# Token mean of the last image on TensorE, and a fixed VectorE order in the choice of experts

## Chip, cores and metric

The kernel runs on one core of a Trainium2 chip. The metric is the device time of one launch in microseconds; the times given are medians over runs. The profile is of one execution, and its times count from the start of its span.

## What is computed

Eight images of 32x32 pixels with 256 channels go through two layers. Layer 0 adds to each image a 3x3 convolution (192 channels) beside an attention with relative positions (64 channels), both of the group-normalised image. Layer 1 is a one-head attention over the 1024 tokens of an image, and then a mixture of experts. What matters here is the seam between those two: the token mean of each normalised image chooses two of eight experts for it.

```python
t = t + _L1_attn_ref(_ln_t(t), ...)
t = t + _L1_ffn_ref(_ln_t(t), ...)
# in _L1_ffn_ref, x being the normalised tokens:
logits = jnp.mean(x, axis=1) @ Wr + br
routing_weights = softmax(logits)
expected_loads = routing_weights.sum(axis=0) * (N / B)
scale = where(expected_loads > capacity, capacity / expected_loads, 1.0)
routing_weights = softmax(routing_weights * scale)
top_w, top_i = top_k(routing_weights, 2); top_w = softmax(top_w)
h = gelu(x @ W1[e] + b1[e]); y = h @ W2[e] + b2[e]
out = layernorm(sum of top_w * y over the two experts + x) * gamma + beta
```

`expected_loads` sums over all eight images, so no image's experts are known before the last image has left the attention of layer 1.

## The kernel before, in words

**Part one** (lines 92 to 1023) goes image by image. An image is a tile `T[b]` of 128 partitions with 8 token groups of 256 channels. `conv_layer_attention` and `attention_layer` do layer 0 and the attention of layer 1; while one image is in `attention_layer`, `fill` feeds TensorE with products of the next image. The last image has no next one, so its `fill` is empty. From line 971 on only TensorE's order is the order in the source (`tc.manual_schedule(engines={PE})`, line 971). On VectorE (DVE), ScalarE (ACT), GpSimd (POOL) and the DMA queues the order is planned at compile time from the dependencies: an instruction whose inputs are ready may be placed ahead of earlier lines. The order is then fixed in the program, and each engine takes its instructions one after the other.

At the end of `attention_layer` for image `b`, `gather` (line 863) and `project` (lines 872 to 881) finish the tokens of the last two groups, and `bn_stats`/`bn_aggr` leave each token's mean and variance in `mv2[:, b, t, :]`. Lines 903 to 909 turn the variances into 1/deviation (`tensor_scalar`, `Sqrt` on ACT, `reciprocal`) and form `mr`, mean times 1/deviation. The token sum `acc`, weighted with 1/deviation, is made by POOL for images 0 to 6 (line 915) and by DVE for image 7 (lines 919 and 921: one `tensor_scalar` and seven `scalar_tensor_tensor` over 256 channels). `T[b]` is stored to `Td[b]` (line 922). `token_mean` (lines 925 to 935) sums `acc` over the partitions with four TensorE passes (line 929, two fp32 products of two passes each), sums `mr` with another product (line 932), reduces it (line 934) and writes the mean, by channel, to `meanT[:, :, b]` (line 935). For images 0 to 6 this runs during the next image; for image 7 it stands alone.

`tab` is a 128x1 tile that serves only to load ACT's function tables early: line 653 computes a `Sqrt` of a late probability tile into it, line 767 an `Exp` of the freshly made deviations.

**The choice of experts** (lines 1054 to 1148) is a chain of tiny operations over 8 images x 8 experts. `plog` is the product with `Wr` (line 1056). `softmax` (lines 1060 to 1069) is a maximum, a subtraction, an `Exp` on ACT, a reciprocal and a multiplication; it is called three times (`sm1`, `sm2`, `sm3`). `pload` sums the loads over the images (line 1075). Then for each of two experts (lines 1092 to 1111): maximum, candidate indices (two operations), minimum, index (line 1099), one-hot row `oh`, the picked weight (lines 1104 and 1105), and the removal of the winner (lines 1108 and 1110). `prow` (line 1120) brings the indices onto one partition, line 1128 casts them to `idx_i`, from which the SP queue reads the addresses for the experts' weights (lines 1155 to 1169). `diag`, `pw` and `wbc` spread the experts' weights over the partitions (lines 1123, 1124, 1130); `dense`, `ptr`, `hotT`, `dbc` (lines 1132 to 1140) make what the biases need, and `pb`, `b1c` (lines 1144, 1148) gather the first bias. All of `plog`, `pload`, `prow`, `pw`, `ptr`, `pb` and later `tp2` take turns in one PSUM pool of two buffers (`ps_t`, tag "t").

**Part two** (lines 1177 to 1256) goes image by image: `load_image` reads `Td[b]` back (line 1152), `n2` normalises it on DVE (line 1189, eight operations of 128x256), TensorE transposes `n2` (line 1196), DVE and ACT copy that to `n2T` (lines 1200 and 1202), TensorE multiplies with `W1` (line 1220), ACT applies `Gelu` (line 1227), TensorE multiplies with the weighted `W2` (line 1237), and DVE and POOL finish the layer norm. Only POOL has its order fixed there.

Of the kernel before, what the change touches and what calls it, by code (L numbers as in the profile page):

```python
# [27 lines left out]
E, F = 8, 512  # L28
NF = F // P
TOPK = 2  # L30
IB = 256
NIB = IB // P
# [4 lines left out]
def kernel(  # L37
# [26 lines left out]
    nc = tc.nc  # L64
# [27 lines left out]
    with ExitStack() as ph:  # L92
        wp = ph.enter_context(tc.tile_pool(name="wp", bufs=1))
        work = ph.enter_context(tc.tile_pool(name="work", bufs=1))
# [25 lines left out]
        def st_tile(name):  # L120
            return ps_st.tile([P, 512], FP, tag="st", name=name)
# [3 lines left out]
        for n, table in (("h", key_rel_h), ("w", key_rel_w)):  # L125
# [21 lines left out]
            out=taps.rearrange("p (n o) -> p n o", o=CO), in_=conv_w.rearrange("a b (k p) o -> p (a b k) o", p=P)  # L147
# [36 lines left out]
        tab = wp.tile([P, 1], FP, tag="tab", name="tab")  # L184
# [573 lines left out]
        def attention_layer(b, fill, whole):  # L758
# [32 lines left out]
            for i in range(2):  # L791
                for q in range(2):
                    pq = st_tile("pq")
                    for kc in range(KC):
                        nc.tensor.matmul(
                            pq,
                            lhsT=wqkv1[:, i, kc, :],
                            rhs=nT[:, kc, q * 512 : (q + 1) * 512],
                            start=kc == 0,
                            stop=kc == KC - 1,  # L800
# [5 lines left out]
            for q in range(2):  # L806
                pv = st_tile("pv1").rearrange("p (j u) -> p j u", u=U)
                for j in range(4):
                    t = q * 4 + j
                    for kc in range(KC):  # L810
                        nc.tensor.matmul(
                            pv[:, j, :],
                            lhsT=nT[:, kc, t * P : (t + 1) * P],
                            rhs=wqkv1[:, 2, kc, :],
                            start=kc == 0,
                            stop=kc == KC - 1,
# [9 lines left out]
            pts = {}  # L826
            st2 = work.tile([P, NT, 6], FP, tag="lst", name="lst2")

            def scores(i):
                lg = lg_tile("lg1")  # L830
                for h in range(2):
                    nc.tensor.matmul(  # L832
                        lg[:, h, :],
                        lhsT=qk[0][:, i * P : (i + 1) * P],
                        rhs=qk[1][:, h * 512 : (h + 1) * 512],
                        start=True,
                        stop=True,
                    )
                lg = lg.rearrange("p h k -> p (h k)")
                nm = work.tile([P, 1], FP, tag="nm", name="nm", bufs=4)  # L840
                nc.vector.tensor_reduce(nm, lg, AX.X, ALU.max, negate=True)  # L841
                nc.vector.tensor_scalar(nm, nm, scale, None, ALU.mult)
                nc.scalar.activation(prs[:, i % 4, :], lg, AF.Exp, bias=nm, scale=scale, accum_out=rs[:, i, :])
# [56 lines left out]
                project(ib, os)  # L900


            m = mv2[:, b]
            rs2 = m[:, :, 1:2]
            nc.vector.tensor_scalar(rs2, rs2, 1e-5, None, ALU.add)
            nc.scalar.activation(rs2, rs2, AF.Sqrt)
            nc.vector.reciprocal(rs2, rs2)
            mr = work.tile([P, NT], FP, tag="mr", name="mr")
            nc.vector.tensor_tensor(mr, m[:, :, 0], m[:, :, 1], ALU.mult)
            acc = work.tile([P, C], FP, tag="n", name="acc", bufs=2)  # L910
            if b + 1 < B:
                part = work.tile([P, C], FP, tag="n", name="part", bufs=2)
                for t in range(NT):
                    to = part if t else acc
                    nc.gpsimd.tensor_scalar(to, T[b][:, t, :], m[:, t, 1:2], None, ALU.mult)
                    if t:
                        nc.gpsimd.tensor_tensor(acc, acc, part, ALU.add)
            else:
                nc.vector.tensor_scalar(acc, T[b][:, 0, :], m[:, 0, 1:2], None, ALU.mult)
                for t in range(1, NT):  # L920
                    nc.vector.scalar_tensor_tensor(acc, T[b][:, t, :], m[:, t, 1:2], acc, ALU.mult, ALU.add)
            nc.gpsimd.dma_start(out=Td[b], in_=T[b])
            return acc, mr

        def token_mean(b, acc, mr):

            pmt = st_tile("pmt")
            for kc in range(KC):
                nc.tensor.matmul(
                    pmt[:, kc : kc + 1], lhsT=acc[:, kc * P : (kc + 1) * P], rhs=ones[:, 0:1], start=True, stop=True  # L930
                )
            nc.tensor.matmul(pmt[:, KC : KC + NT], lhsT=ones, rhs=mr, start=True, stop=True)
            mrs = work.tile([P, 1], FP, tag="mrs", name="mrs")
            nc.vector.tensor_reduce(mrs, pmt[:, KC : KC + NT], AX.X, ALU.add)
            nc.vector.tensor_scalar(meanT[:, :, b], pmt[:, 0:KC], mrs, 1.0 / S, ALU.subtract, ALU.mult)

        class Conv:

# [106 lines left out]
    iota_i = small.tile([B, E], I32, tag="iota_i", name="iota_i")  # L1045
    nc.gpsimd.iota(iota_i, pattern=[[1, E]], base=0, channel_multiplier=0)
    iota = small.tile([B, E], FP, tag="iota", name="iota")
    nc.vector.tensor_copy(iota, iota_i)

    def sm(shape, name):  # L1050
        return small.tile(shape, FP, tag=name, name=name)
# [8 lines left out]
    def softmax(dst, src, name):  # L1060
# [7 lines left out]
        nc.vector.tensor_scalar(dst, dst, s, None, ALU.mult)  # L1068
        return d

    rw = sm([B, E], "rw")
    softmax(rw, logits, "sm1")

# [8 lines left out]
    z = sm([B, E], "z")  # L1082
# [8 lines left out]
    hot = []  # L1091
    for k in range(TOPK):
        m = sm([B, 1], f"m{k}")
        nc.vector.tensor_reduce(m, z, AX.X, ALU.max)
        cand = sm([B, E], f"cand{k}")
        nc.vector.tensor_scalar(cand, z, m, -float(E), ALU.is_equal, ALU.mult)
        nc.vector.tensor_tensor(cand, cand, iota, ALU.add)
        nc.vector.tensor_reduce(idx[:, k : k + 1], cand, AX.X, ALU.min)
        nc.vector.tensor_scalar(idx[:, k : k + 1], idx[:, k : k + 1], float(E), float(E - 1), ALU.add, ALU.min)
        oh = sm([B, E], f"oh{k}")  # L1100
        nc.vector.tensor_scalar(oh, iota, idx[:, k : k + 1], None, ALU.is_equal)
        hot.append(oh)
        pick = sm([B, E], f"pick{k}")
        nc.vector.tensor_tensor(pick, oh, rw2, ALU.mult)
        nc.vector.tensor_reduce(top[:, k : k + 1], pick, AX.X, ALU.add)
        if k + 1 < TOPK:
            off = sm([B, E], f"off{k}")
            nc.vector.tensor_scalar(off, oh, 4.0, None, ALU.mult)
            z2 = sm([B, E], f"z{k}")
            nc.vector.tensor_tensor(z2, z, off, ALU.subtract)  # L1110
            z = z2
    wt = sm([B, TOPK], "wt")
    softmax(wt, top, "sm3")


    prow = ps_t.tile([P, 512], FP, tag="t", name="prow")
    pw = ps_t.tile([P, 512], FP, tag="t", name="pw")
    diag = sm([B, TOPK, B], "diag")
    for k in range(TOPK):
        nc.tensor.matmul(  # L1120
            prow[0:1, k * B : (k + 1) * B], lhsT=idx[:, k : k + 1], rhs=ident[0:B, 0:B], start=True, stop=True
        )
        nc.vector.tensor_scalar(diag[:, k, :], ident[0:B, 0:B], wt[:, k : k + 1], None, ALU.mult)
    nc.tensor.matmul(
        pw[:, 0 : TOPK * B], lhsT=ones[0:B], rhs=diag.rearrange("p k b -> p (k b)"), start=True, stop=True
    )
    idx_i = small.tile([1, TOPK * B], I32, tag="idx_i", name="idx_i")
    nc.vector.tensor_copy(idx_i, prow[0:1, 0 : TOPK * B])
    wbc = sm([P, TOPK * B], "wbc")
    nc.vector.tensor_copy(wbc, pw[:, 0 : TOPK * B])  # L1130
    dense = sm([B, E], "dense")
# [14 lines left out]
        )  # L1146
    b1c = sm([P, NF, TOPK * B], "b1c")
    nc.vector.tensor_copy(b1c, pb)

    def load_image(b):  # L1150
        t = work.tile([P, NT, C], FP, tag="T2", name="T2")
        nc.sync.dma_start(out=t, in_=Td[b])
        return t

    def load_experts(b):
        ws = []
# [20 lines left out]
    ctx.enter_context(tc.manual_schedule(engines={mybir.EngineType.Pool}))  # L1177
    nxt = load_experts(0)
    scale_experts(0, nxt)
    tn = load_image(0)  # L1180
    for b in range(B):
        ws, Tb = nxt, tn
        if b + 1 < B:
            tn = load_image(b + 1)
            nxt = load_experts(b + 1)
        n2 = work.tile([P, NT, C], FP, tag="n2", name="n2")
        n2T = work.tile([P, KC, S], FP, tag="n2T", name="n2T")
        for t in range(NT):
            nc.vector.tensor_scalar(
                n2[:, t, :], Tb[:, t, :], mv2[:, b, t, 0:1], mv2[:, b, t, 1:2], ALU.subtract, ALU.mult  # L1190
            )
        for kc in range(KC):
            for q in range(2):
                tp = ps_t.tile([P, 4, P], FP, tag="t", name="tp2")
# [112 lines left out]
```

## Time and profile before

| | us |
|---|---|
| median of 3 runs (2446.56 to 2452.04) | 2448.43 |
| the profiled execution's own time | 2444.67 |
| its span | 2442.9 |
| TensorE busy in the span | 2314.1 (95%) |
| VectorE busy | 1485.5 (61%) |
| ScalarE busy | 1026.1 (42%) |
| GpSimd busy | 475.6 (19%) |

In the timeline a row gives the start, the busy time, engine and line, the operation with the tiles it writes and reads, how many were merged, and in brackets how long the engine was idle before it and whose result it waited for. "PE" is a matmul, "PEld" a weight load that overlaps it. An fp32 product appears as two passes ("x2"). In a table by stretches, each engine's busy time and its number of instructions stand side by side, then the clock that TensorE was granted (1.00 is full speed), the busy share of the DMA engines and GB/s.

### The profile page before, as it was taken

How to read it: one execution, taken by the hardware profiler on the slowest of the kernel's cores; microseconds unless marked ns; L12 is line 12 of the kernel's file. 1: busy time of each engine (PE TensorE's matmuls, PEld its weight loads, DVE VectorE, ACT ScalarE, POOL GpSimd, SP SyncE). 2: the span in 40 equal slices, each digit the busy share in tenths (PEclk: the TensorE clock that was granted, in tenths of full speed). 3: DMA queues.
4: the chain of work that ended last, by engine and by line, in shares of the span. 5: the costliest groups of instructions: out<-in, count | busy, mean ns of one | idle time of the engine just before them, and what ended most of it. 6: DMA issues, size and time to landing. Idle time of an engine off the chain costs nothing. (4 is left out here: it accounts for less than half of the span.)

```text
span 2442.9 us, 41840 instructions
## 1 busy us (share of the span) xinstructions
PE 2314.1 (95%) x17273; PEld 1299.7 (53%) x17273; DVE 1485.5 (61%) x2661; ACT 1026.1 (42%) x1717; POOL 475.6 (19%) x446
## 2 busy tenths in 40 slices
PE   5999999999999999999999999999998879999998
PEld 4535643564366436643663376337632546666665
DVE  7776487548755875587467746774774434444443
ACT  2255336433643464346335732563266323222232
POOL 3202130213031202210230023002301032222221
PEclk7999999999999999999999999999999989999999
DMA  4521242134222412240324032403240032121210
GB/s 124 82 40 27 41 97 39 35 46 90 32 43 57 80 22 51 57 85 9 58 70 72 4 57 70 72 4 57 60 66 2 23 121 69 69 69 69 70 60 26
DMA packets 71468, 135.82 MB, mean 56 GB/s; under 512 B 12000, under 2 KB 24168, under 8 KB 69232
## 3 DMA queue, kind: packets, MB, share of 16 engines
q1 hardware_dynamic: 65488, 115.47, 23.7%
q0 software_dynamic: 3056, 15.73, 1.9%
q8 instruction: 136, 2.23, 0.4%
q10 hardware_dynamic: 2736, 1.97, 0.3%
q14 instruction: 52, 0.43, 0.1%
HBM read 53.43 MB, written 25.17 MB: 32 GB/s over the span
## 5 line engine op out<-in xcount | busy, mean ns | idle before, releaser
L591 DVE TENSOR_REDUCE my<-lg 128x32 f32<-128x1024 f32 x512 | 618.5, 1223 | 161.8 <-PE st L623 125.9
L631 ACT ACTIVATE PT<-st 128x512 f32<-128x512 f32 (+1 forms) x944 | 541.6, 633 | 306.2 <-PE st L623 301.7
L623 PE MATMUL st<-F,km 32*128 32x512 f32 x2048 | 545.2, 641 | 17.2 <-DMA F<-mb 11.9
L583 PE MATMUL lg<-km,F 24*128 24x512 f32 x2048 | 534.9, 637 | 6.1 <-DMA F<-kq 3.7
L640 PE MATMUL po<-PT,vall 128*32 128x256 f32 (+1 forms) x3200 | 315.1, 453 | 2.9 <-ACT PT L631 2.4
L583 PEld LDWEIGHTS lg<-km,F 24*128 24x128 f32 x2048 | 156.0, 183 | 186.5 <-issue 112.1
L515 PE MATMUL pc<-convw,gdif 128*128 128x192 f32 x1152 | 236.1, 345 | 11.5 <-ACT m L524 8.7
L640 PEld LDWEIGHTS po<-PT,vall 128*32 128x32 f32 x3200 | 66.9, 108 | 314.6 <-issue 280.1
L515 PEld LDWEIGHTS pc<-convw,gdif 128*128 128x128 f32 x1152 | 186.8, 192 | 81.5 <-issue 59.9
L623 PEld LDWEIGHTS st<-F,km 32*128 32x128 f32 x2048 | 177.5, 184 | 96.3 <-issue 43.5
L1220 PE MATMUL phd<-n2T,w 128*128 128x512 f32 x512 | 223.7, 594 | 0.0
L1237 PE MATMUL py<-w,hT 128*128 128x256 f32 x1024 | 223.6, 379 | 0.0
L1237 PEld LDWEIGHTS py<-w,hT 128*128 128x128 f32 x1024 | 194.6, 190 | 33.3 <-issue 7.4
L311 POOL TENSOR_TENSOR T<-T,l0b 128x2048 f32<-128x2048 f32 x8 | 36.4, 4546 | 633.5 <-PE tpx L304 633.5
L1220 PEld LDWEIGHTS phd<-n2T,w 128*128 128x128 f32 x512 | 97.0, 191 | 114.9 <-issue 107.7
L1244 DVE TENSOR_TENSOR r<-py,n 128x256 f32<-128x256 f32 x64 | 27.1, 423 | 215.0 <-PE py L1237 215.0
L863 PE MATMUL po<-pt,qkv 128*128 128x256 f32 x512 | 116.6, 381 | 11.3 <-DVE pt L855 11.3
L524 ACT COPY m<-pc 128x384 f32<-128x384 f32 x48 | 23.0, 479 | 247.3 <-PE pc L515 247.3
L1227 ACT ACTIVATE hT<-phd,b1c 128x512 f32<-128x512 f32 x128 | 86.3, 686 | 96.5 <-PE phd L1220 96.3
L841 DVE TENSOR_REDUCE nm<-lg 128x1 f32<-128x1024 f32 x64 | 78.1, 1220 | 77.5 <-PE lg L832 77.5
L780 POOL TENSOR_TENSOR T<-T,n 128x256 f32<-128x256 f32 x64 | 47.1, 743 | 372.8 <-DVE n L775 372.8
L832 PE MATMUL lg<-qkv 128*128 128x512 f32 x256 | 119.1, 593 | 0.0
(250 smaller groups left out, 2627.6 us busy)
## 6 DMA issues: line engine op xcount, KB each, us to landing
F<-rh SPq DMA_DIRECT2D x256, 128.0 KB
F<-kq SPq DMA_DIRECT2D x256, 64.0 KB
F<-rwd SPq DMA_DIRECT2D x256, 64.0 KB
w<-in_L_ffn_W_dram SPq DMA_DIRECT2D x32, 512.0 KB
rwd<-rw SPq DMA_DIRECT2D x16, 512.0 KB
Td<-T POOLq DMA_DIRECT2D x8, 1024.0 KB, 8.3
T<-Td SPq DMA_DIRECT2D x8, 1024.0 KB
out_dram<-yo SPq DMA_DIRECT2D x16, 512.0 KB
```

Source lines behind the costliest of these rows:

```text
L515: nc.tensor.matmul(pc[:, v, :], lhsT=gflat[:, 2 * pair + v, kc, at : at + P], rhs=convw[:, 2 * pair + v, dy, kc * CO : (kc + 1) * CO], sta ...
L583: nc.tensor.matmul(lg[:, a, :], lhsT=self.F[r : r + 24, a, 0, i * P : (i + 1) * P], rhs=KM[self.g][r : r + 24, a].rearrange("p e k -> p (e ...
L591: nc.vector.tensor_reduce(my[:, :, hl], lg.rearrange("p a (y x) -> p y a x", y=WW), AX.XY, ALU.max)
L623: nc.tensor.matmul(st[:, i, :] if len(heads) > 1 else st, lhsT=KM[self.g][r : r + 32, a, e, :], rhs=self.F[r : r + 32, a, e, :], start=Tru ...
L631: nc.scalar.activation(self.pts[j][:, hs, :], st, AF.Exp)
L640: nc.tensor.matmul(self.po[32 * hl : 32 * hl + 32, cols], lhsT=vall[:, j, h * (DH + 1) : h * (DH + 1) + 32], rhs=self.pts[j][:, hl, cols], ...
L832: nc.tensor.matmul(lg[:, h, :], lhsT=qk[0][:, i * P : (i + 1) * P], rhs=qk[1][:, h * 512 : (h + 1) * 512], start=True, stop=True,)
L841: nc.vector.tensor_reduce(nm, lg, AX.X, ALU.max, negate=True)
L863: nc.tensor.matmul(po[:, 0:IB], lhsT=v1[:, jc, :], rhs=pt[:, jc, :], start=jc == 0, stop=jc == NT - 1)
L1220: nc.tensor.matmul(phd, lhsT=ws[k][0][:, kc, f * P : (f + 1) * P], rhs=n2T[:, kc, q * 512 : (q + 1) * 512], start=kc == 0, stop=kc == KC - 1,)
L1227: nc.scalar.activation(hT[:, k * NF + f, :], phd, AF.Gelu, bias=b1c[:, f, k * B + b : k * B + b + 1])
L1237: nc.tensor.matmul(py, lhsT=hT[:, k * NF + f, j * P : (j + 1) * P], rhs=ws[k][1][:, f, :], start=k == 0 and f == 0, stop=k == TOPK - 1 and ...
```

## The change

For image 7 the weighted token sum is a product on TensorE: token group as stationary operand, the column of 1/deviation as moving operand, summed over the eight groups in PSUM, in two halves of channels. The deviations are made in two parts, groups 0 to 5 and groups 6 and 7. After it an `Exp` from `tab` to `tab` stands in the source. `token_mean` writes `meanT` with one operation for each half of the channels, for all images. In the choice of experts, DVE's order is that of the source from the first softmax to `b1c`; the candidates take one operation instead of two, the removal of the winner one instead of two, the index is made after the one-hot row, the picked weights, `sm3`, `pw` and what follows stand after `idx_i` and after the normalisation of image 0, which is now called there. `load_image(0)` is called ahead of the first softmax.

```diff
+            def deviation(part):
+                m = mv2[:, b, part]
+                rs2 = m[:, :, 1:2]
+                nc.vector.tensor_scalar(rs2, rs2, 1e-5, None, ALU.add)
+                nc.scalar.activation(rs2, rs2, AF.Sqrt)
+                nc.vector.reciprocal(rs2, rs2)
+                nc.vector.tensor_tensor(mr[:, part], m[:, :, 0], m[:, :, 1], ALU.mult)
...
             if b + 1 < B:
+                deviation(slice(0, NT))
...
             else:
-                nc.vector.tensor_scalar(acc, T[b][:, 0, :], m[:, 0, 1:2], None, ALU.mult)
-                for t in range(1, NT):
-                    nc.vector.scalar_tensor_tensor(acc, T[b][:, t, :], m[:, t, 1:2], acc, ALU.mult, ALU.add)
+                acc = [st_tile(f"pm{kc}") for kc in range(KC)]
+                for part in (slice(0, NT - NIB), slice(NT - NIB, NT)):
+                    deviation(part)
+                    for t in range(part.start, part.stop):
+                        for kc in range(KC):
+                            nc.tensor.matmul(
+                                acc[kc][:, 0:1],
+                                lhsT=T[b][:, t, kc * P : (kc + 1) * P],
+                                rhs=mv2[:, b, t, 1:2],
+                                start=t == 0,
+                                stop=t == NT - 1,
+                            )
+                nc.scalar.activation(tab, tab, AF.Exp)
             nc.gpsimd.dma_start(out=Td[b], in_=T[b])
...
-            nc.vector.tensor_scalar(meanT[:, :, b], pmt[:, 0:KC], mrs, 1.0 / S, ALU.subtract, ALU.mult)
+            for kc in range(KC):
+                nc.vector.tensor_scalar(
+                    meanT[:, kc, b : b + 1], acc[kc][:, 0:1], mrs, 1.0 / S, ALU.subtract, ALU.mult
+                )
...
-    nc.vector.tensor_copy(iota, iota_i)
+    nc.vector.tensor_scalar(iota, iota_i, -float(E), None, ALU.add)
...
+    tn = load_image(0)
...
+    order = tc.manual_schedule(engines={mybir.EngineType.DVE})
+    order.__enter__()
     rw = sm([B, E], "rw")
     softmax(rw, logits, "sm1")
...
-        nc.vector.tensor_scalar(cand, z, m, -float(E), ALU.is_equal, ALU.mult)
-        nc.vector.tensor_tensor(cand, cand, iota, ALU.add)
-        nc.vector.tensor_reduce(idx[:, k : k + 1], cand, AX.X, ALU.min)
-        nc.vector.tensor_scalar(idx[:, k : k + 1], idx[:, k : k + 1], float(E), float(E - 1), ALU.add, ALU.min)
+        nc.vector.scalar_tensor_tensor(cand, z, m, iota, ALU.is_equal, ALU.mult)
+        low = sm([B, 1], f"low{k}")
+        nc.vector.tensor_reduce(low, cand, AX.X, ALU.min)
         oh = sm([B, E], f"oh{k}")
-        nc.vector.tensor_scalar(oh, iota, idx[:, k : k + 1], None, ALU.is_equal)
+        nc.vector.tensor_scalar(oh, iota, low, None, ALU.is_equal)
...
-            nc.vector.tensor_scalar(off, oh, 4.0, None, ALU.mult)
-            nc.vector.tensor_tensor(z2, z, off, ALU.subtract)
+            nc.vector.scalar_tensor_tensor(z2, oh, -4.0, z, ALU.mult, ALU.add)
             z = z2
+        nc.vector.tensor_scalar(idx[:, k : k + 1], low, float(E), float(E - 1), ALU.add, ALU.min)
...
+    nc.vector.tensor_copy(idx_i, prow[0:1, 0 : TOPK * B])
+    first = normalised(0, tn)
+    for k, oh in enumerate(hot):
+        nc.vector.tensor_tensor(pick, oh, rw2, ALU.mult)
+        nc.vector.tensor_reduce(top[:, k : k + 1], pick, AX.X, ALU.add)
+    softmax(wt, top, "sm3")
...
     b1c = sm([P, NF, TOPK * B], "b1c")
     nc.vector.tensor_copy(b1c, pb)
+    order.__exit__(None, None, None)
...
-    tn = load_image(0)
     for b in range(B):
...
+        n2 = normalised(b, Tb) if b else first
```

`normalised(b, Tb)` holds the eight operations that stood at line 1189. In `token_mean` the product of line 929 is kept for images 0 to 6; image 7 reads the two PSUM columns of the new product, and its `pmt` lies in the other PSUM pool (`lg_tile`).

More of the change, by code (lines that the diff above doesn't have):

```diff
@@ L827, in attention_layer @@
             st2 = work.tile([P, NT, 6], FP, tag="lst", name="lst2")
+            mr = work.tile([P, NT], FP, tag="mr", name="mr")
+            def deviation(part):
[5 more added lines that the diff above has]
+                nc.vector.tensor_tensor(mr[:, part], m[:, :, 0], m[:, :, 1], ALU.mult)
             def scores(i):
@@ L900, in attention_layer @@
                 project(ib, os)
[L903 to L910, printed above, removed]
             if b + 1 < B:
+                deviation(slice(0, NT))
+                acc = work.tile([P, C], FP, tag="n", name="acc", bufs=2)
                 part = work.tile([P, C], FP, tag="n", name="part", bufs=2)
@@ L914, in attention_layer @@
                     to = part if t else acc
-                    nc.gpsimd.tensor_scalar(to, T[b][:, t, :], m[:, t, 1:2], None, ALU.mult)
+                    nc.gpsimd.tensor_scalar(to, T[b][:, t, :], mv2[:, b, t, 1:2], None, ALU.mult)
                     if t:
@@ L925, in token_mean @@
         def token_mean(b, acc, mr):
[L927 to L931, printed above, removed]
+            pmt = lg_tile("pmt")[:, 0, :] if b + 1 == B else st_tile("pmt")
+            if b + 1 < B:
+                for kc in range(KC):
+                    nc.tensor.matmul(
+                        pmt[:, kc : kc + 1], lhsT=acc[:, kc * P : (kc + 1) * P], rhs=ones[:, 0:1], start=True, stop=True
+                    )
+                acc = [pmt[:, kc : kc + 1] for kc in range(KC)]
             nc.tensor.matmul(pmt[:, KC : KC + NT], lhsT=ones, rhs=mr, start=True, stop=True)
@@ L934, in token_mean @@
             nc.vector.tensor_reduce(mrs, pmt[:, KC : KC + NT], AX.X, ALU.add)
-            nc.vector.tensor_scalar(meanT[:, :, b], pmt[:, 0:KC], mrs, 1.0 / S, ALU.subtract, ALU.mult)
+            for kc in range(KC):
+                nc.vector.tensor_scalar(
+                    meanT[:, kc, b : b + 1], acc[kc][:, 0:1], mrs, 1.0 / S, ALU.subtract, ALU.mult
+                )
         class Conv:
@@ L1047, with load_image, normalised @@
     iota = small.tile([B, E], FP, tag="iota", name="iota")
-    nc.vector.tensor_copy(iota, iota_i)
+    nc.vector.tensor_scalar(iota, iota_i, -float(E), None, ALU.add)
+    def load_image(b):
+        t = work.tile([P, NT, C], FP, tag="T2", name="T2")
+        nc.sync.dma_start(out=t, in_=Td[b])
+        return t
+    def normalised(b, Tb):
+        n2 = work.tile([P, NT, C], FP, tag="n2", name="n2")
+        for t in range(NT):
+            nc.vector.tensor_scalar(
+                n2[:, t, :], Tb[:, t, :], mv2[:, b, t, 0:1], mv2[:, b, t, 1:2], ALU.subtract, ALU.mult
+            )
+        return n2
+    tn = load_image(0)
     def sm(shape, name):
@@ L1095 @@
         cand = sm([B, E], f"cand{k}")
-        nc.vector.tensor_scalar(cand, z, m, -float(E), ALU.is_equal, ALU.mult)
-        nc.vector.tensor_tensor(cand, cand, iota, ALU.add)
-        nc.vector.tensor_reduce(idx[:, k : k + 1], cand, AX.X, ALU.min)
-        nc.vector.tensor_scalar(idx[:, k : k + 1], idx[:, k : k + 1], float(E), float(E - 1), ALU.add, ALU.min)
+        nc.vector.scalar_tensor_tensor(cand, z, m, iota, ALU.is_equal, ALU.mult)
+        low = sm([B, 1], f"low{k}")
+        nc.vector.tensor_reduce(low, cand, AX.X, ALU.min)
         oh = sm([B, E], f"oh{k}")
-        nc.vector.tensor_scalar(oh, iota, idx[:, k : k + 1], None, ALU.is_equal)
+        nc.vector.tensor_scalar(oh, iota, low, None, ALU.is_equal)
         hot.append(oh)
-        pick = sm([B, E], f"pick{k}")
-        nc.vector.tensor_tensor(pick, oh, rw2, ALU.mult)
-        nc.vector.tensor_reduce(top[:, k : k + 1], pick, AX.X, ALU.add)
         if k + 1 < TOPK:
-            off = sm([B, E], f"off{k}")
-            nc.vector.tensor_scalar(off, oh, 4.0, None, ALU.mult)
             z2 = sm([B, E], f"z{k}")
-            nc.vector.tensor_tensor(z2, z, off, ALU.subtract)
+            nc.vector.scalar_tensor_tensor(z2, oh, -4.0, z, ALU.mult, ALU.add)
             z = z2
-    wt = sm([B, TOPK], "wt")
-    softmax(wt, top, "sm3")
+        nc.vector.tensor_scalar(idx[:, k : k + 1], low, float(E), float(E - 1), ALU.add, ALU.min)
     prow = ps_t.tile([P, 512], FP, tag="t", name="prow")
-    pw = ps_t.tile([P, 512], FP, tag="t", name="pw")
-    diag = sm([B, TOPK, B], "diag")
     for k in range(TOPK):
@@ L1122 @@
         )
+    idx_i = small.tile([1, TOPK * B], I32, tag="idx_i", name="idx_i")
+    nc.vector.tensor_copy(idx_i, prow[0:1, 0 : TOPK * B])
+    first = normalised(0, tn)
+    for k, oh in enumerate(hot):
+        pick = sm([B, E], f"pick{k}")
+        nc.vector.tensor_tensor(pick, oh, rw2, ALU.mult)
+        nc.vector.tensor_reduce(top[:, k : k + 1], pick, AX.X, ALU.add)
+    wt = sm([B, TOPK], "wt")
+    softmax(wt, top, "sm3")
+    pw = ps_t.tile([P, 512], FP, tag="t", name="pw")
+    diag = sm([B, TOPK, B], "diag")
+    for k in range(TOPK):
         nc.vector.tensor_scalar(diag[:, k, :], ident[0:B, 0:B], wt[:, k : k + 1], None, ALU.mult)
@@ L1126 @@
     )
-    idx_i = small.tile([1, TOPK * B], I32, tag="idx_i", name="idx_i")
-    nc.vector.tensor_copy(idx_i, prow[0:1, 0 : TOPK * B])
     wbc = sm([P, TOPK * B], "wbc")
@@ L1148 @@
     nc.vector.tensor_copy(b1c, pb)
[L1150 to L1153, printed above, removed]
+    order.__exit__(None, None, None)
     def load_experts(b):
@@ L1185 @@
             nxt = load_experts(b + 1)
-        n2 = work.tile([P, NT, C], FP, tag="n2", name="n2")
+        n2 = normalised(b, Tb) if b else first
         n2T = work.tile([P, KC, S], FP, tag="n2T", name="n2T")
[L1188 to L1191, printed above, removed]
         for kc in range(KC):
```

## Prediction

> **What bounds the kernel now.** First the page.
>
> ```profile
> span 2442.9 us, 41840 instructions
> PE 2314.1 (95%) x17273; PEld 1299.7 (53%) x17273; DVE 1485.5 (61%) x2661; ACT 1026.1 (42%) x1717; POOL 475.6 (19%) x446
> PEclk7999999999999999999999999999999989999999
> ```
>
> TensorE is the bound nearly everywhere. The change touches places where it isn't, so I cut the span into stretches of 40 us (columns: PE, PEld, DVE, ACT, POOL, then clock).
>
> ```profile
> 1920.00:1960.00 40.00, 26.54 (x128) 19.76 (x126) 22.14 (x64) 11.94 (x21) 0.74 (x2) 0.89 0.20 67
> 1960.00:2000.00 40.00, 31.80 (x110) 20.91 (x111) 13.97 (x59) 10.20 (x17) 20.56 (x8) 0.77 0.36 126
> 2000.00:2040.00 40.00, 40.00 (x149) 26.67 (x148) 16.41 (x37) 12.38 (x19) 5.51 (x3) 1.00 0.20 66
> ```
>
> From 2000 on PE is full up to the end, so whatever lets its stream of part two begin earlier is kept to the end. Between 1946 and 1969 it waits for a chain of small steps. The timeline there:
>
> ```profile
> 1941.23 3.72 PE L863 MATMUL po<-pt,qkv 128*128 128x256 f32 x16 [1.41 <-DVE pt L855]
> 1945.43 1.28 ACT L906 ACT_TABLE_LOAD   x1
> 1946.64 0.88 DVE L879 SCALAR_TENSOR_TENSOR T<-pa,rc,T 128x256 f32<-128x256 f32 x2 [5.37 <-PE pa L875]
> 1948.90 0.20 DVE L907 RECIPROCAL mv<-mv 128x8 f32<-128x8 f32 x1 [0.28 <-ACT mv L906]
> 1949.60 3.61 DVE L921 SCALAR_TENSOR_TENSOR acc<-T,mv,acc 128x256 f32<-128x256 f32 x7
> 1953.36 0.98 PE L929 MATMUL pmt<-ones,acc 128*128 128x1 f32 x4 [6.76 <-DVE acc L921]
> 1954.81 0.17 DVE L934 TENSOR_REDUCE mrs<-pmt 128x1 f32<-128x8 f32 x1 [1.60 <-PE pmt L932]
> 1956.47 1.28 ACT L1066 ACT_TABLE_LOAD   x1 [7.60 <-DVE sm_d L1065]
> 1960.93 0.41 DVE L1189 TENSOR_SCALAR n<-T,mv 128x256 f32<-128x256 f32 x1
> 1965.20 0.15 DVE L1128 CAST idx_i<-prow 1x16 int32<-1x16 f32 x1
> 1967.90 0.35 DVE L1123 TENSOR_SCALAR diag<-ident,wt 8x8 f32<-8x8 f32 x2
> 1969.26 1.88 PE L1144 MATMUL pb<-hotT,b1sb 8*128 8x16 f32 x8 [0.28 <-DVE hotT L1138]
> 1971.07 1.11 PE L1196 MATMUL tp<-ident,n 128*128 128x128 f32 x4
> ```
>
> Three pieces stand in the chain: the weighted sum on DVE (1949.2 to 1953.2), the table load ahead of the first exponential, and the choice. In the choice, normalisations of line 1189 are wedged between its steps: from 1960.93 to 1967.7 I count sixteen, image 0's eight and then image 1's. From `pb` at 1969.26 PE is busy without a pause. That start is what the change can move.
>
> The experts' weights aren't late: SP issues the first load 1.22 after `idx_i` (1966.57); by the DMA rates it lands around 1970.5, an estimate, and the product using it starts at 1975.0.
>
> **What the Trainium skill says.** "ScalarE: Activation LUTs", section "What ACT_TABLE_LOAD costs", gives 1283 ns for the load; the trace agrees (1.28). The page adds a drain of 1380 ns, which I don't see: the exponential starts at 1957.76, right behind the load. "TensorE: Matmul & The Clock Gate", section "LDWEIGHTS (loading the stationary operand)", lets a weight load depend on its columns alone, columns/1.2 ns, 107 for 128. The trace agrees at full clock:
>
> ```profile
> 1644.52 1.90 PE L417 MATMUL pvv<-qkvw,x 128*128 128x64 f32 x16
> ```
>
> With 0.275 for the last one that is 0.11 a pass; at half clock `pb` takes 0.235. The same page, "What's actually happening", halves the clock after an idle window of about 3.4 us. Here it falls at 1950.7, 4.1 after the last product of line 875, and is full again only at 1978.1.
>
> **Part 1, the mean by PE.** Removed: line 919 (0.35), line 921 (3.61) and line 929's four passes, 1953.36 to 1954.2. Added: 16 products, 32 passes, in PE's fixed order behind line 875. Groups 0 to 5 have their variances at 1941.26, and DVE and ACT idle then, so their deviations should be ready before PE is free at about 1946.4. Their 24 passes take 24 x 0.11 = 2.6, to 1949.05. Groups 6 and 7 follow the same DVE steps as now; reciprocal done at 1949.1. Eight passes, 0.9, to 1950.05, line 932's two with their tail 0.35: line 934 starts at 1950.45 instead of 1954.81. Minus 4.35. `meanT` takes a second small operation: plus 0.13 (two of line 1123 take 0.35). Net 4.2.
> Bounds: were the square root of the first part planned behind the copy of line 867, its table load ends at 1946.7 and I lose 0.8. Were the first part to wait for all eight variances, 32 x 0.11 = 3.5 begin at 1949.15 and the gain is 1.7. Were the clock to fall earlier, 0.11 becomes 0.235, the sum ends at 1953.9, line 932 takes 0.6, and the gain is 0.2.
>
> **Part 2, the table.** If the new `Exp` of `tab` runs after the second square root, the load of 1.28 at 1956.47 leaves the chain. But it reads only `tab`, last written at line 767 (1886.7); ACT's order isn't fixed, and ACT idles 1.90 just after. That the planner pulls ready work far ahead is seen in line 1189: image 1's normalisation, a whole image further down the source, runs inside the choice. I take it that the `Exp` goes up there, under a table that is Exp's anyway, and brings 0. Bounds: 0 and minus 1.3.
>
> **Part 3, the choice.** I count from the end of `sm2`'s subtraction, 1960.0, in steps seen undisturbed: 0.18 to 0.19 for a dependent small operation (1958.98 to 1959.78), 0.25 with a per-row scalar. The fixed order puts `sm2`'s reciprocal and scaling, which wait for ACT, ahead of the maximum: it starts at +0.79, now +0.03. Then five dependent steps for the first expert, to +1.90; four for the second, index ready at +2.73; `prow` and cast, `idx_i` at +3.25, now +5.35. So 2.1 earlier, but only for weights that aren't late.
> For `pb` the order costs: eight normalisations in a row, 2.7 (line 1189's group of eight at 2050.71 takes 2.67), to +5.95; picked weights 0.6; `sm3` with its ACT trip 1.25; `diag` at +7.8 (now +7.9). Then `wbc` is in front of `dense` and waits for `pw`, about 0.6, where `dense` now fills that wait; `dense`, `ptr`, `hotT` end at +9.8, `pb` starts at +9.86 instead of +9.26. Loss 0.6. PE's transposes don't get ahead: `tp2` shares the two PSUM buffers in turn, and even now `n2` of four groups is ready at 1962.7 while its transposes run at 1971.07.
> Queued behind: behind the cast sits DVE's normalisation, which needs image 0 back from `Td`. SP's load waited for the store (until 1952.6), then for `meanT` (1955.2); now the store is last, so it issues about 1952.7 and lands, by today's issue at 1955.37 and first use at 1960.93, by 1958.2 at the latest. It is wanted at 1959.05: no wait, 0.9 to spare; past that each us counts. SP's other DMAs keep their order: two image loads, then the experts; POOL's only change is `Td`'s store, still behind line 879.
> Image 1's eight normalisations lose their free place. They lie under TensorE's stream (DVE idles 18.5 before 1994.45), unless the planner puts some ahead of the copies of line 1200 or into the last steps: 0 to 2.7, I take 0.5.
>
> **Part 4, images 0 to 6.** One more small DVE operation each, 7 x 0.13 = 0.9 if DVE were the bound; PE is full there, so 0.2, bounds 0 and 0.9.
>
> **Sum.** 4.2 - 0.6 - 0.5 - 0.2 = 2.9 off the path. Against the profiled execution: 2444.67 to 2441.8, span 2442.9 to 2440.0. That execution is 3.8 below the runs' median; from 2448.43 the same step gives 2445.5.
>
> **Rivals.**
> A, likeliest, as summed: 2445.5.
> B, the table does come ahead: 1.3 more, 2444.2. For it: ACT also idles after the second root. Against it: nothing ties it there.
> C, the mean isn't ready early (dependency on all variances, or half clock): gain 1.7 or 0.2, about 1.0 for 4.2, leaves the total at about 2448.7, no change. For it: the clock falls at 1950.7, just behind my end of 1950.4.
> D, slower. Images differ now: line 907 comes every 239.1 for images 1 and 2 and every 237.5 for images 3 to 5. At the end of layer 0's attention the longer ones show a stretch at half clock:
>
> ```profile
> 442.00:444.00 2.00, 2.00 (x12) 0.25 (x10) 2.00 (x6) 1.94 (x4) 0.00 (x0) 0.53 0.00 0
> ```
>
> The extra operation and the new dependencies let the planner re-order DVE and ACT in images 0 to 6; if four more of them meet that, 4 x 1.6 = 6.4 against 2.9: 2451.9. It decides from two images on. Against it: PE's order is fixed there, and the change is tiny in that part.
>
> **Numbers.** A 0.46, B 0.29, C 0.15, D 0.10. What a measurement can tell from no change is about 0.2%, 4.9 us: below 2443.5 or above 2453.3. Medians of a few runs scatter by some 2 us (2446.56 to 2452.04 before). A falls below 2443.5 in 0.09 of its 0.46, B in 0.14 of 0.29, C in 0.02: faster 0.25. D is above 2453.3 in half of its 0.10, C and A in 0.01: slower 0.06. Within: 0.69. The range goes from B with the best mean and nothing lost in parts 3 (image 1) and 4 (gain 5.0 and one scatter: 2441.4) to C with a scatter (2450.7).
>
> **What would show it.** Right: line 934 about 4.3 earlier relative to line 879; a table load still in front of the first exponential of the choice; `idx_i` about 3.3 after `sm2`'s subtraction; `pb` about 9.9 after it. Wrong: no table load there (B); PE waiting for deviations or 0.2 a pass (C); DVE waiting for `T` from `Td`, or image 1's normalisations between `hotT` and the copies; longer periods of line 907 (D).

## The result, and the profile after

| | before | after |
|---|---|---|
| median, 22 runs each | 2451.10 | 2445.64 |
| lowest, highest | 2443.42, 2453.03 | 2440.24, 2449.88 |
| profiled execution's own time | 2444.67 | 2449.88 |
| its span | 2442.9 | 2448.1 |

The ratio is 0.9983 [0.9975, 0.9992]: the change takes off 4.2 us, between 2.0 and 6.1, by 2451.1. The runs of either kernel fall into groups: 2443.4 to 2443.8, 2446.5 and 2450.6 to 2453.0 before, 2440.2 to 2441.2, 2442.6 to 2444.2 and 2447.1 to 2449.9 after. Group against group the change brings about 3, and the medians differ by 5.5 because 13 of 22 runs before and 11 of 22 after lie in the highest group. The profiled execution after is its kernel's slowest run, so spans can't be compared. I compare the seam instead.

Lines have moved: 879 became 890, 934 became 950, 1066 became 1101, 1128 became 1151, 1189 became 1078, 1144 became 1183, 1196 became 1226, 1220 became 1250. First the page of the kernel after.

```profile
span 2448.1 us, 41896 instructions
PE 2325.5 (95%) x17301; PEld 1304.1 (53%) x17301; DVE 1482.9 (61%) x2661; ACT 1027.0 (42%) x1719; POOL 476.2 (19%) x446
PEclk7999999999999999999999999999999989999999
```

PE is busy 11.4 longer than before, far more than the 28 new records of passes can take. That is a clock, not work; I come back to it. Now the timeline of the seam after the change.

```profile
1950.07 0.21 ACT L836 ACTIVATE mv<-mv 128x6 f32<-128x6 f32 x1
1954.75 3.73 PE L929 MATMUL pm<-mv,T 128*128 128x1 f32 x32
1954.95 0.88 DVE L890 SCALAR_TENSOR_TENSOR T<-pa,rc,T 128x256 f32<-128x256 f32 x2 [4.25 <-PE pa L886]
1958.74 0.17 DVE L950 TENSOR_REDUCE mrs<-pmt 128x1 f32<-128x8 f32 x1 [1.18 <-PE pmt L948]
1958.94 0.34 DVE L952 TENSOR_SCALAR meanT<-pm,mrs 128x1 f32<-128x1 f32 x2
1960.27 1.28 ACT L1101 ACT_TABLE_LOAD   x1 [3.10 <-DVE sm_d L1100]
1963.58 0.22 DVE L1100 TENSOR_SCALAR sm_d<-z,sm_m 8x8 f32<-8x8 f32 x1
1966.72 0.16 DVE L1151 CAST idx_i<-prow 1x16 int32<-1x16 f32 x1 [0.29 <-PE prow L1147]
1967.00 2.67 DVE L1078 TENSOR_SCALAR n<-T,mv 128x256 f32<-128x256 f32 x8
1970.28 0.39 DVE L1078 TENSOR_SCALAR n<-T,mv 128x256 f32<-128x256 f32 x1
1970.73 0.72 DVE L1078 TENSOR_SCALAR n<-T,mv 128x256 f32<-128x256 f32 x2
1974.27 0.17 DVE L1177 COPY hotT<-ptr 8x24 f32<-8x24 f32 x1
1974.48 1.30 DVE L1179 COPY dbc<-hotT 8x1024 f32<-8x1024 f32 x1
1974.50 1.88 PE L1183 MATMUL pb<-hotT,b1sb 8*128 8x16 f32 x8 [0.26 <-DVE hotT L1177]
```

From the start of line 890 the mean's reduction (950) comes after 3.79; line 934 came 8.17 after line 879. By its 0.12 a pass, the 24 passes of the first six groups are about done when the last two deviations arrive, and the deviations of the first part were ready at 1950.5, four ahead of PE. The table load still stands before the first exponential. `idx_i` is there 3.08 after the second softmax's subtraction ends (1963.80; in this document "the subtraction"). Then the eight normalisations run in one piece, image 1's follow between the small steps (three of its eight shown), and `pb` comes 10.70 after the subtraction, where it was 9.26. Before, that subtraction stood here:

```profile
1959.78 0.22 DVE L1065 TENSOR_SCALAR sm_d<-z,sm_m 8x8 f32<-8x8 f32 x1
```

Here and in the table of the experiments S is the time from the start of the last line 879 or 890 to the start of `pb`, and E to the end of the first 32 products of line 1220 or 1250. Before, S is 22.62 and E 44.25; after, 19.55 and 41.06. So the seam is 3.07 shorter at its middle and 3.19 at its end, and what follows takes as long as before (from the start of the last line 879 or 890 to the end of the span: 496.26 and 493.10, 3.16 apart).

What hides this gain in the spans is the start of that line, 1946.64 before and 1954.95 after. The sum closes: 2444.67 + 8.31 - 3.1 = 2449.9. Most of the 8.31 arises in images 3 to 7, in code that the change hardly touches. Compare a stretch of 40 us at the end of layer 0's attention of image 3 (the third number from the right is the clock), first before:

```profile
920.00:960.00 40.00, 38.12 (x580) 26.01 (x577) 24.68 (x71) 17.95 (x29) 8.48 (x12) 1.00 0.15 40
```

and after:

```profile
920.00:960.00 40.00, 38.44 (x512) 24.60 (x512) 25.64 (x72) 17.94 (x27) 6.84 (x9) 0.96 0.11 28
444.00:445.00 1.00, 1.00 (x7) 0.00 (x0) 1.00 (x4) 1.00 (x3) 0.00 (x0) 0.50 0.00 0
```

The second of these lines is 1 us of such a place in image 1: a clock of 0.50, which lasts some 3.4 us (443.70 to 447.11) and lengthens an image from 237.5 to about 239. Before, the profiled execution has this in two images (1 and 2), after in all of 1 to 7. By the starts of lines 907 and 837, 5.7 of the 8.31 arise in images 3 to 6 and 1.0 in image 7. The other 1.6 are there at 200 us already (line 327's first load starts at 201.27 in place of 199.69), from the first 80 us, where the clock goes up and down in both.

### The profile page after: what moved, and what is told of

It reads as the page before. It is cut to its first block, busy times and chain, and to the rows that moved or that the text cites. A ratio compares the mean times of both kernels' runs of the same rounds, so it can differ in the third digit from the quotient of the medians.

```text
span 2448.1 us, 41896 instructions
## 1 busy us (share of the span) xinstructions
PE 2325.5 (95%) x17301; PEld 1304.1 (53%) x17301; DVE 1482.9 (61%) x2661; ACT 1027.0 (42%) x1719; POOL 476.2 (19%) x446
```

## The experiments

Edits are shown against the kernel after. The times of the experiments come with a median of the kernel before on the same chip: 2447.05 (37 runs) for the first four experiments, 2451.5 (36 runs) for the others. The lowest run of before is 2443.3 to 2443.8 in each of these sets and in that of the change, so I set lowest beside lowest too. By the ratio only choice alone is clearly apart from the change; the intervals of the others touch or overlap its own. What ranks them is S, from one profiled execution each, and the lowest runs follow it to within 1.2 us.

E holds one thing more than S: after the chain of small steps TensorE starts at half clock, and full speed comes back between 7.8 us (mean and table) and 10.9 us (both) after the start of `pb`. So S measures the edits, and E adds some luck.

| kernel | S | E | ratio [95%] | lowest |
|---|---|---|---|---|
| before | 22.62 | 44.25 | 1 | 2443.4 |
| the change | 19.55 | 41.06 | 0.9983 [0.9975, 0.9992] | 2440.2 |
| mean alone | 15.72 | 37.41 | 0.9973 [0.9962, 0.9984] | 2437.7 |
| choice alone | 25.32 | 47.52 | 1.0014 [1.0005, 1.0023] | 2447.3 |
| tied table | 22.22 | 43.82 | 1.0001 [0.9992, 1.0009] | 2443.4 |
| free order | 16.18 | 37.69 | 0.9972 [0.9963, 0.9980] | 2436.6 |
| weights first | 14.56 | 36.84 | 0.9963 [0.9948, 0.9979] | 2436.0 |
| table kept | 17.98 | 40.35 | 0.9979 [0.9970, 0.9988] | 2439.8 |
| both | 13.28 | 35.93 | 0.9959 [0.9942, 0.9976] | 2434.2 |
| mean and table | 13.55 | 34.75 | 0.9961 [0.9945, 0.9976] | 2434.6 |

**Mean alone.** Part one of the change, with the choice of experts as it was before.

```diff
-    order = tc.manual_schedule(engines={mybir.EngineType.DVE})
-    order.__enter__()
...
-        nc.vector.scalar_tensor_tensor(cand, z, m, iota, ALU.is_equal, ALU.mult)
+        nc.vector.tensor_scalar(cand, z, m, -float(E), ALU.is_equal, ALU.mult)
+        nc.vector.tensor_tensor(cand, cand, iota, ALU.add)
...
-    first = normalised(0, tn)
...
-        n2 = normalised(b, Tb) if b else first
+        n2 = work.tile([P, NT, C], FP, tag="n2", name="n2")
```

> The mean by TensorE alone (with the Exp of tab), the choice of experts as before. Measure: from the start of the last image's last scale-and-add on DVE (T<-pa,rc,T of groups 6 and 7) to the start of pb; 22.62 us before, 19.55 after the whole change. Mine (the mean gains 4.3, the choice gives 1.3 back): 18.3, better than the whole change. Rival (the gain comes from the choice, the mean only trades DVE time for TensorE passes): 21 to 22.6.

S is 15.72: this part gains 6.9, not the 4.3 that was expected of it. Of these, 4.5 lie ahead of the end of the subtraction (8.84 after the start of line 890, where it was 13.36), and 2.4 behind it. The timeline shows the second share.

```profile
1955.33 0.22 DVE L1084 TENSOR_SCALAR sm_d<-z,sm_m 8x8 f32<-8x8 f32 x1
1958.54 0.16 DVE L1147 CAST idx_i<-prow 1x16 int32<-1x16 f32 x1
1959.45 0.41 DVE L1208 TENSOR_SCALAR n<-T,mv 128x256 f32<-128x256 f32 x1
1962.43 1.89 PE L1163 MATMUL pb<-hotT,b1sb 8*128 8x16 f32 x8 [0.26 <-DVE hotT L1157]
```

With the old instructions, in the planner's order, `idx_i` is ready 3.15 after the subtraction instead of 5.35. No normalisation is placed ahead of it any more: the first starts at 1959.45, after the cast. Before, ten were wedged in ahead of the cast and six more ahead of `pb`; now six in all stand ahead of `pb`. So 2.2 of the old choice's 5.35 were not its own instructions but what was put between them, and the edit of part one was enough to undo that. Why the planner places them otherwise now, the record doesn't show.

**Choice alone.** Part one as before, with the new choice.

```diff
-                acc = [st_tile(f"pm{kc}") for kc in range(KC)]
-                for part in (slice(0, NT - NIB), slice(NT - NIB, NT)):
-                    deviation(part)
...
+                nc.vector.tensor_scalar(acc, T[b][:, 0, :], m[:, 0, 1:2], None, ALU.mult)
+                for t in range(1, NT):
+                    nc.vector.scalar_tensor_tensor(acc, T[b][:, t, :], m[:, t, 1:2], acc, ALU.mult, ALU.add)
```

> The choice of experts alone (fewer instructions, DVE's order fixed, normalisation of image 0 in front of the picked weights), mean on DVE as before. Same measure. Mine: 23.9, slower than before by 1.3, although idx_i comes about 2 us earlier after the second softmax's subtraction. Rival: about 20, most of the gain.

S grows by 2.7, and the kernel is slower than before, by a ratio of 1.0014. `idx_i` is early here too (3.08 after the subtraction), but `pb` stands behind sixteen normalisations, at 11.96 after it. The fixed choice is a loss by itself; its sign was forecast, its size is twice the 1.3 expected. Of the excess of 1.4, one operation accounts for 0.86:

```profile
1965.49 2.67 DVE L1059 TENSOR_SCALAR n<-T,mv 128x256 f32<-128x256 f32 x8
1972.64 5.99 POOL L1191 TENSOR_SCALAR w<-w,wbc 128x1024 f32<-128x1024 f32 x2 [21.92 <-DVE wbc L1150]
1972.69 1.07 DVE L1153 SCALAR_TENSOR_TENSOR dense<-oh,wt,dense 8x8 f32<-8x8 f32 x1
1974.23 0.68 DVE L1160 COPY dbc<-hotT 8x1024 f32<-8x1024 f32 x1
1974.25 1.88 PE L1164 MATMUL pb<-hotT,b1sb 8*128 8x16 f32 x8 [0.26 <-DVE hotT L1158]
```

The second half of `dense`, 0.21 in the change, takes 1.07 here. It starts 0.05 after GpSimd begins to scale the experts' weights, and the way to `pb` leads over it.

**Tied table.** The new `Exp` reads a deviation of the last group, so it can't run early.

```diff
-                nc.scalar.activation(tab, tab, AF.Exp)
+                nc.scalar.activation(tab, mv2[:, b, NT - 1, 1:2], AF.Exp)
```

> The whole change, with the Exp into tab reading the last deviations instead of tab, so that it can't run before the last square root. Mine: no table load in front of the choice's first exponential, measure 18.3 (19.55 less 1.28), or up to 0.7 more if image 0 coming back from Td becomes the next thing waited for, since it is loaded at a time set by the store. Rival (the Exp of tab did run late, and something else reloads the table): the load stays, 19.5.

The load of the table leaves the chain: it runs at 1947.85, and none stands at line 1101. But nearly the whole gain of the change is gone, S being 22.22, which neither the expectation nor its rival had. The waits of the SP queue and the timeline show why. (In a row of waits: total, how often, longest.)

```profile
SPq L1053 <- ACT tab L936: 3.8, 1, 3.8
```

```profile
1951.57 0.24 PE L1091 MATMUL plog<-wr,meanT 128*8 128x8 f32 x4 [2.20 <-DMA wr<-in_L_ffn_Wr_dram]
1960.33 2.67 DVE L1078 TENSOR_SCALAR n<-T,mv 128x256 f32<-128x256 f32 x8 [2.46 <-DMA T<-Td]
```

The first load of the choice, `wr`, is issued 3.83 after the start of line 890, in place of 0.12, because its place was held until `tab` was read for the last time: the tiles of part two reuse what part one leaves. `plog` waits 2.20 for it. The five loads behind it on SP are late too. Image 0 is issued only 0.3 later than in the change (6.70 after line 890 against 6.43), but DVE waits 2.46 for it and starts 8.04 after its issue, where 5.62 was enough in the change. That it lands so late because six other loads were issued just ahead of it may be the reason; it isn't shown.

**Free order.** The change without its fixed order on DVE.

```diff
-    order = tc.manual_schedule(engines={mybir.EngineType.DVE})
-    order.__enter__()
...
-    order.__exit__(None, None, None)
```

> The whole change without the fixed DVE order in the choice: fewer instructions, planned freely. Mine (the fixed order is what gives back, since the picked weights stand behind eight normalisations): idx_i later, pb earlier; measure 17 to 18.3. Rival (the fixed order is what gains): idx_i and pb both later, measure 20.5 to 21.5.

S is 16.18, 3.4 better than with the order and below the range expected. `idx_i` is not later, as I expected, but earlier: 2.46 after the subtraction (end at 1958.25). The fewer instructions are worth 0.7 against the 3.15 of the old ones, and the fixed order had eaten 0.6 of that, by putting `sm2`'s reciprocal and scaling ahead of the maximum. What stands in front of `pb` here, and not in the mean alone, is one choice of the planner's:

```profile
1962.09 0.21 DVE L1169 TENSOR_SCALAR dense<-oh,wt 8x8 f32<-8x8 f32 x1
1962.23 2.65 DVE L1078 TENSOR_SCALAR n<-T,mv 128x256 f32<-128x256 f32 x8
1964.88 0.20 DVE L1170 SCALAR_TENSOR_TENSOR dense<-oh,wt,dense 8x8 f32<-8x8 f32 x1
```

All eight of image 0's normalisations run between the two halves of `dense`, and `pb` comes 7.33 after the subtraction, against 6.88 in the mean alone.

**Weights first.** The order is fixed still, but the picked weights and `sm3` stand ahead of the normalisations, `dense` ahead of `wbc`, and the eight are spread over the places where DVE waits for PE. `idx_i` is cast while `sm3`'s exponential runs, and `dbc` comes last.

```diff
-    nc.vector.tensor_copy(idx_i, prow[0:1, 0 : TOPK * B])
-    first = normalised(0, tn)
+    first = work.tile([P, NT, C], FP, tag="n2", name="n2")
...
-    wbc = sm([P, TOPK * B], "wbc")
-    nc.vector.tensor_copy(wbc, pw[:, 0 : TOPK * B])
...
+    normalised(0, tn, first, range(0, 1))
...
     nc.vector.tensor_copy(hotT, ptr[0:E, 0 : (TOPK + 1) * B])
+    normalised(0, tn, first, range(1, 4))
+    wbc = sm([P, TOPK * B], "wbc")
+    nc.vector.tensor_copy(wbc, pw[:, 0 : TOPK * B])
+    normalised(0, tn, first, range(4, NT))
```

> The whole change with another fixed order: picked weights and the third softmax right behind the second one-hot row, the normalisation of image 0 spread behind dense and hotT (one operation, then three, then four), dense ahead of wbc, dbc last. Same measure as before. If the loss is that eight normalisations stand in front of the weights and image 1's wedge in behind them: pb 6 after the second softmax's subtraction instead of 10.7, measure 14.8, time 4 to 5 below the whole change. Rival (pb then waits for something else, image 0 or the biases): 17 to 19.

```profile
1962.95 0.22 DVE L1101 TENSOR_SCALAR sm_d<-z,sm_m 8x8 f32<-8x8 f32 x1
1968.88 1.89 PE L1189 MATMUL pb<-hotT,b1sb 8*128 8x16 f32 x8 [0.27 <-DVE hotT L1181]
```

`pb` stands 5.71 after the subtraction in place of 10.70, and S is 14.56. `idx_i` comes later than in the change (3.64 against 3.08), and it costs nothing that is seen. A fixed order wasn't wrong as such; what it had in front was.

**Table kept.** The tied `Exp` again, with `tab` in a pool that lives to the end.

```diff
-        tab = wp.tile([P, 1], FP, tag="tab", name="tab")
+        tab = keep.tile([P, 1], FP, tag="tab", name="tab")
...
-                nc.scalar.activation(tab, tab, AF.Exp)
+                nc.scalar.activation(tab, mv2[:, b, NT - 1, 1:2], AF.Exp)
```

> The whole change with the Exp into tab reading the last deviations, and tab in the pool that part two doesn't reuse, so that the loads of wr and the others need not wait for that Exp. If the reuse of tab's place was what took the table's gain away: wr is issued as in the whole change, no table load in the chain, measure 18.3, up to 0.7 more where image 0 lands after the index is cast. Rival (TensorE's product with wr waits for its landing anyway, or all of the gain goes to the wait for image 0): 19.5.

```profile
1945.85 0.41 SPq L1053 DMA_DIRECT2D wr<-in_L_ffn_Wr_dram  x1
1948.06 1.28 ACT L936 ACT_TABLE_LOAD   x1
1951.16 0.21 ACT L1101 ACTIVATE rw<-sm_d 8x8 f32<-8x8 f32 x1 [1.60 <-DVE sm_d L1100]
1957.32 2.67 DVE L1078 TENSOR_SCALAR n<-T,mv 128x256 f32<-128x256 f32 x8 [0.85 <-DMA T<-Td]
```

`wr` goes out at once, the load runs early, and S falls from 19.55 to 17.98, by 1.57. This confirms the reading of the tied table: the wait was for the tile's place. Of the 1.57, 1.28 lie ahead of the end of the subtraction and are the table's; 0.29 lie behind it. The chain is now short enough that image 0's load is last, by 0.85. At E only 0.71 of the 1.57 is left, since full clock comes back 10.2 after the start of `pb`, against 8.6 in the change. The median (2447.25) looks poor beside the lowest run (2439.8); 11 of its 20 runs lie in its highest group. So by the times of the runs this kernel can't be told from the change.

**Both, and mean with table.** The first is weights first with the kept table, the second the mean alone with it; their diffs are those above.

> The order of e5 with the table of e6. If both hold and nothing else becomes last: measure 13.5, time 6 below the whole change. If image 0 coming back becomes last (it lands up to 5.6 after its issue, and its issue waits for the store): the normalisation waits 0.5 to 2, measure 13.5 all the same, but TensorE's stream behind pb starts later by that much.

> The mean alone (choice as before, planned freely) with the table of e6. If the table is worth 1.28 there too: measure 14.4 against 15.72 with the mean alone. Rival: planned freely, image 0's normalisations land earlier in the plan and wedge into the choice again, measure 16 to 18.

```profile
1961.66 1.88 PE L1163 MATMUL pb<-hotT,b1sb 8*128 8x16 f32 x8 [0.28 <-DVE hotT L1157]
1961.71 0.41 DVE L1208 TENSOR_SCALAR n<-T,mv 128x256 f32<-128x256 f32 x1
```

S is 13.28 and 13.55. Both are about 0.4% under the kernel before, and their lowest runs lie 6.0 and 5.6 under that of the change. In the first the table brings exactly 1.28 (14.56 to 13.28). In the second S falls by 2.17: 1.28 ahead of the end of the subtraction, and 0.89 because the planner now places no normalisation at all ahead of `pb`; the first, in the lines above, starts just after it. That is the opposite of the rival. By the ratio I can't tell the two kernels apart. E is shorter in the second by 1.2, though its S is longer by 0.3. Its first 32 products take 14.4 against 16.0, as full clock came back earlier. The second needs nothing of the new choice at all.

## Why the prediction was right or wrong

**Part 1, the mean.** Right: line 950 comes 4.38 earlier relative to the scale-and-add (4.35 forecast), and `meanT` takes 0.12 more (0.13). The 32 passes take 3.73, 0.12 each. Neither of C's causes is seen: the first deviations were early, and the passes ran at full clock. Not forecast were another 0.25: in two operations, `meanT` is half ready early, and the product with `Wr` starts at 1959.26, just before the second half ends (1959.28), where it started 0.26 after the end before.

**Part 2, the table.** Right, as A had it against B. The list of the line's runs after the change:

```profile
L767 ACT ACTIVATE tab<-lmv x8: 203/203/203, 231.2 to 1895.0; 128x1 f32<-128x1 f32 x8
L936 ACT ACTIVATE tab<-tab x1: 202/202/202, 1895.2 to 1895.2; 128x1 f32<-128x1 f32 x1
```

The `Exp` runs at 1895.2, right behind line 767's last, 66 us ahead of the exponential that it was to serve. Tied and kept, it takes 1.28 off the way to the subtraction in all three kernels that have it so (table kept, both, mean and table), which is the bound of 1.3. The Trainium skill, "ScalarE: Activation LUTs", section "What ACT_TABLE_LOAD costs", has 1283 ns for the load, which agrees, and adds a drain of 1380 ns for every switch; a gain of 1.28 leaves no room for it, and the measurement decides.

**Part 3, the choice.** The direction was right, two sizes were off a little. `idx_i` came 3.08 after the subtraction (3.25 forecast). For `pb` the forecast was a loss of 1.1; it was 1.44. Image 1's did not stay out of the last steps: all eight lie between 1970.28 and 1974.34, inside my bounds of 0 to 2.7 but above the 0.5. DVE did not wait for image 0, as forecast.

What the step did not see is whose gain the early `idx_i` was. I set the new order against "now +5.35" and took the 2.1 between as its doing. The mean alone reaches +3.15 with the old instructions and no order. I had said that the planner pulls ready work ahead, but kept its placing when I moved the mean, although that placing changes with small edits: sixteen normalisations stand ahead of `pb` before, six in the mean alone, none in the mean with the table. So there is no one price of a part. The mean brings 6.9 beside the old choice (22.62 to 15.72) and 5.8 beside the new one (25.32 to 19.55); the new choice costs 2.7 beside the old mean and 3.8 beside the new.

The sum was not hurt by this, as it set both parts together against the kernel before. There the way to the end of the subtraction became shorter by 4.51 (13.36 to 8.85), for 4.2, and the rest to `pb` longer by 1.44, for 1.1. Two misses of 0.3 cancel, and that is luck: 3.1 measured at the seam, and 3.1 forecast for it.

**Part 4, images 0 to 6.** Nothing is seen of the seven small operations. An image without the half clock takes 237.5 before and 237.5 in the mean alone, which has the same part one as the change; one with it takes 239.1 before and 238.95 after.

**The sum.** A step of 2.9 was forecast; the seam shows 3.1, group against group shows about 3, and the ratio 4.2 with an interval that holds them. That the median 2445.64 lies next to 2445.5 is partly luck: the median of before moved from 2448.43 in three runs to 2451.10 in twenty-two.

**Rival D.** Its sign appeared in the profile, the longer images at a half clock, but its cause is not needed. The mean alone, free order and weights first have the part one of the change, line for line, and meet the half clock in two, three and seven images; before has it in two, the change in seven. The profiles with seven (the change and weights first) reach the last line 879 or 890 at 1954.95 and 1954.32, the one with five (both) at 1950.90, those with two or three at 1945.6 to 1949.4. Not every difference among the last is explained, and that the planner left images 0 to 6 as they were was not tested by itself.

## What to carry to other kernels

When a chain is shortened at its head, a planner's order further down has to be read anew: what was wedged into the chain may leave it by itself, and a fixed order written against the old wedging can then cost more than it saves. In a fixed order, put bulk work only behind the last small step that another engine waits for. An early table load needs an operand that exists only when the table is wanted, and a tile whose place nobody waits for.

## What the runs showed of the hardware

**A half clock that comes and goes.** At the end of layer 0's attention TensorE pauses for 0.75 between products of 32 rows, in each of images 0 to 6 and in before as in the change. In some images its clock then falls to 0.50 for 3.4 us, in others not. Before, image 1 and then image 6, each with 2 us behind its pause (the third number from the right is the clock):

```profile
440.69 1.13 PE L623 MATMUL st<-F,km 32*128 32x512 f32 x6 [0.75 <-ACT PT L631]
442.00:444.00 2.00, 2.00 (x12) 0.25 (x10) 2.00 (x6) 1.94 (x4) 0.00 (x0) 0.53 0.00 0
1631.40 1.13 PE L623 MATMUL st<-F,km 32*128 32x512 f32 x6 [0.75 <-ACT PT L631]
1632.00:1634.00 2.00, 2.00 (x18) 0.50 (x16) 2.00 (x7) 2.00 (x4) 0.00 (x0) 1.00 0.00 0
```

So the pause alone doesn't decide it. The Trainium skill, "TensorE: Matmul & The Clock Gate", section "What's actually happening", speaks of a free-running window of 3413 ns. In the change line 837 starts at 310.60, 549.65, 788.72, 1027.68, 1266.62, 1505.55 and 1744.49: the last four periods are 238.93 to 238.96, and 70 windows are 238.91, an estimate by that page's figure. Images without the half clock take 237.5, which is no whole number of windows. So an image that meets it puts the next image's pause at nearly the same place of a window, and the next tends to meet it too. It need not last: before has it in images 1 and 2 and not in 3 to 6, the tied table in 4 and 5 and not in 6. This fits the groups of times, but it is argued from periods; no run tested it.

**DVE operations held up beside GpSimd.** `dbc` (8x1024, line 1179) takes 1.30 in the change, where GpSimd scales the weights at the same time (from 1973.68), and 0.67 in the mean alone and in weights first, where GpSimd starts after it. But in choice alone `dbc` takes 0.68 with GpSimd at work, and there it is the small second half of `dense` that takes 1.07 in place of 0.21. In both runs one operation near GpSimd's start is longer, by 0.63 and 0.86, and others beside it are not. What decides which one is open; it was not measured by itself.
